# Splitting three of the last product's seven half-size products once more, in a float32 RWKV attention and Hadamard feed-forward kernel

## The chip, the cores and the metric

The kernel runs on one core of a Trainium2 chip, in float32 throughout. The metric is the device time of one execution in microseconds (us): the median over repeated runs. A profiled execution gives a trace of every instruction of the five engines: TensorE (PE, with its weight loads PEld), VectorE (DVE), ScalarE (ACT), GpSimd (POOL) and SyncE (SP), which issues all DMAs here.

## The reference, cut to what matters

```python
xn = _layernorm(x)                                   # x: 4 batches x 2048 tokens x 512 channels
r, k, v = (einsum(mix(xn, mu), W) for r, k, v)       # 512 x 512 each; mix = mu * x + (1 - mu) * the token before
attn = einsum(sigmoid(r) * wkv_recurrence(k, v, w, u), Wo)
up = silu(einsum(xn, W1)) * einsum(xn, W3)           # 512 -> 2048
ffn = einsum(fwht(up), W2)                           # Walsh-Hadamard over 2048, then 2048 -> 512
out = x + attn + ffn
```

The last step of each part is a product onto the same 512 channels. The kernel folds the Hadamard transform into `W2` once, puts `Wo` below it, and so computes one last product with 2048 + 512 = 2560 rows.

## The kernel before, in words

The 8192 tokens are worked in 8 blocks of `TB` = 1024 tokens. Within a block there are three stages on TensorE: the r, k and v projections, 16 turns of `up` (each makes 128 of the 2048 hidden channels for all 1024 tokens), and `down`, the last product. Meanwhile VectorE and ScalarE work through the recurrence (`wkv`, given out piece by piece by `step`).

Every product is done by the seven-product form of a 2 x 2 matrix product (Strassen-Winograd): weights and tokens are cut into halves, sums and differences of the quarters are made ("forms"), and seven products of half size take the place of eight. The forms of the weights are made by GpSimd in the first block and kept in DRAM (`part_w`, `down_w`). In `down` the contraction is cut into the halves kh (ten tiles of 128 rows each: eight of `hid`, two of `r_sb`), the output channels into the halves mh (two tiles of 128, index g), the tokens into two halves of 512. `y11`, `y12`, `y21`, `y22` are the quarters of the right-hand side (first index kh, second the token half). One of the seven products is 2 x 10 matmuls of 128 x 128 weights on 512 columns; a float32 matmul shows in the trace as two passes, each with its own weight load.

The order of work on each engine is the order of the program text (`InOrder`), and SP's queue is one such list for all DMAs. `product(k, ...)` inside `down` first issues the load of the weights of product k + 1 (1280 KB, into a ring `ring_b` of two slots), then lets the generator `between` do one part of the next block's preparation (`next_tokens`: statistics of the tokens, `normalize`, the mixed inputs `mixed` and their forms `mix_forms`), then issues its 20 matmuls. The differences of the y quarters stand between the products on VectorE, written in place. `normalize` gives two of the four channel tiles to VectorE and two to GpSimd. In the first block, `down_parts` and `down_forms` make the forms of the last product's weights during the first ten turns of `up`.

`pa`, `pb`, `pc` are PSUM banks that sums grow in; `act.copy` starts a second bank with what has been summed so far. `stage` and `x22_of` hold the residual x, which sums are added onto before they are stored. The last product of the last block is cut into two halves of 256 columns.

Of the kernel before, what the change touches and what calls it, by code (L numbers as in the profile page):

```python
# [14 lines left out]
P = 128  # L15
# [24 lines left out]
def tile_rwkv_attn_hadamard_ffn(  # L40
# [20 lines left out]
    NR = (NF + NB) // 2  # L61
    n_blocks = NT // TB
# [6 lines left out]
    ring_b = ctx.enter_context(tc.tile_pool(name="ring_b", bufs=2))  # L69
# [6 lines left out]
    down_w = dram.tile([7, P, NR, KH, P], F32, name="down_w")  # L76
# [3 lines left out]
    hid = const.tile([P, NF, TB], F32, name="hid")  # L80
    xnT = const.tile([P, NB, OFF + TB], F32, name="xnT")
    tf = const.tile([P, 4, KH, H], F32, name="tf")
    r_sb, k_sb, v_sb = (const.tile([P, NB, TB], F32, name=n) for n in ("r_sb", "k_sb", "v_sb"))
# [3 lines left out]
    turn = [0]  # L87

# [8 lines left out]
    u2_of = [e1b[:, ts(g, H)] for g in range(KH)]  # L97
    x22_of = [e1[:, ts(g, H)] for g in range(KH)]
    mix_of = {1: tf.rearrange("p f k t -> p (f k t)").rearrange("p (b t) -> p b t", t=TB)}
    mix_of[2], mix_of[0] = hid[:, 0:NB, :], hid[:, NB : 2 * NB, :]  # L100
    t4_of = {kind: hid[:, NF // 2 + n, :] for n, kind in enumerate((1, 2, 0))}
# [43 lines left out]
    def normalize():  # L145
        for b in range(NB):
            eng = dve if b < KH else pool
            for s, op in ((0, ALU.mult), (1, ALU.add)):
                xb = xnT[:, b, OFF : OFF + TB]
                eng.tensor_tensor(xb, xb, spread[:, s, :], op)  # L150
# [52 lines left out]
    def load_square(i, kind):  # L203
        t = ring_b.tile([P, NB, C], F32, tag="b", name=f"w_{i}_{kind}")
        sp.dma_start(out=t, in_=wrkv[kind])
        return t

    def projected(kind, w, h, half):
        pt = bank()
        for b in range(NB):  # L210
            pe.matmul(
                pt, lhsT=w[:, b, ts(h, P)], rhs=mix_of[kind][:, b, ts(half, H)], start=(b == 0), stop=(b == NB - 1)
            )
        dst = (r_sb, k_sb, v_sb)[kind][:, h, ts(half, H)]
        if kind == 0:
            act.activation(dst, pt, AF.Tanh, scale=0.5)
        else:
            act.copy(dst, pt)


    def wkv(h):
        w_h, u_h = weff[:, h : h + 1], vec[:, 4, h : h + 1]
        r, k, v = r_sb[:, h, :], k_sb[:, h, :], v_sb[:, h, :]
# [67 lines left out]
    def mix_forms(kind):  # L291

        m11, m12, m21, m22 = quarters(mix_of[kind], 0)
        if kind == 1:
            f1, f2 = (by_tile(s[:, OFF : OFF + TB]) for s in (sa, sb))
        else:
            slot = ring_b.tile([P, 2, KH, H], F32, tag="b", name=f"mf_{kind}")
            f1, f2 = slot[:, 0], slot[:, 1]
        f4 = by_tile(t4_of[kind])
        right_of[kind] = (m11, m21, m22, f1, f2, m12, f4)  # L300
        for out, x, y in ((f1, m12, m11), (f2, m22, f1), (m12, m22, m12), (f4, m21, f2)):
            dve.tensor_tensor(out, x, y, ALU.subtract)
            yield
# [61 lines left out]
    def projected_pair(i, n, w, tail, hook):  # L365
# [3 lines left out]
        dst = (r_sb, k_sb, v_sb)[kind]  # L369
        d11, d12, d21, d22 = (dst[:, mh * KH + g, ts(t, H)] for mh in range(2) for t in range(2))  # L370
# [25 lines left out]
    def up(i, j, w, tail, step):  # L396

        keep_parts(i, 3 * KH + j, w)
        h0, h1 = hid[:, j, 0:H], hid[:, j, H:TB]
# [24 lines left out]
    NP = NF // 2  # L424
    fold = [hid[:, NP + n, :] for n in range(NP)]

# [37 lines left out]
    def down_parts(n):  # L464
        t = ring_b.tile([P, 7, KH, P], F32, tag="b", name=f"df_{n}")
        if n >= NP:
            sp.dma_start(out=t[:, 0:4], in_=wo[n - NP])
        return t

    def down_forms(j, at, t):  # L470
        n, a = at[j] if j < NP else (j, None)
        far = down_w[:, :, n].rearrange("f p k c -> p f k c")
        if n < NP:
            a = a.rearrange("p (k m g c) -> p k m g c", k=2, m=2, c=P)
            seven_forms([t[:, f] for f in range(4)], a[:, 0, 0], a[:, 1, 0], a[:, 1, 1], a[:, 0, 1])
            sp.dma_start(out=far[:, 0], in_=a[:, 0, 0])
            sp.dma_start(out=far[:, 1:3], in_=a[:, 1])
            sp.dma_start(out=far[:, 3:7], in_=t[:, 0:4])
        else:
            forms_in(t)  # L480
            sp.dma_start(out=far, in_=t)

    def load_down(i, form):
        t = ring_b.tile([P, NR, KH, P], F32, tag="b", name=f"dw_{i}_{form}")
        sp.dma_start(out=t, in_=down_w[form])
        return t

    def rows(kh, half):

        n = NF // 2  # L490
        pieces = [hid[:, kh * n + 2 * a : kh * n + 2 * a + 2, ts(half, H)] for a in range(n // 2)]
        return pieces + [r_sb[:, kh * KH : (kh + 1) * KH, ts(half, H)]]

    order = (0, 1, 4, 6, 5, 3, 2)

    def down(i, w, between, w_after, last):
        y11, y12, y21, y22 = rows(0, 0), rows(0, 1), rows(1, 0), rows(1, 1)
        def product(k, pts, right, start, then):
            if k == 6:
                w_after()  # L500
            elif k:
                w.append(load_down(i, order[k + 1]))
            if k:
                next(between)
            for g in range(KH):
                whole = slice(0, H)
                for pt, cols in ending if last and k == 6 and g == KH - 1 else [(pts[g], whole)]:
                    for n in range(NR):
                        pe.matmul(
                            pt[:, cols], lhsT=w[k][:, n, g, :], rhs=right[n // 2][:, n % 2, cols],  # L510
                            start=start and n == 0, stop=n == NR - 1, skip_group_check=True,
                        )
                    then(g) if cols == whole else c21(g, pt, cols)

        def difference(out, x0, x1):
            for o, p0, p1 in zip(out, x0, x1):
                dve.tensor_tensor(o, p0, p1, ALU.subtract)
# [4 lines left out]
        def residual(slot, mh, g, half):  # L522
            c, t = at(mh, g, half)
            sp.dma_start(out=slot, in_=xT[c, t])

        def store(slot, mh, g, half):
            c, t = at(mh, g, half)
            sp.dma_start(out=outT[c, t], in_=slot)

        add = dve.tensor_tensor  # L530
        pa, pb, pc = ([bank() for _ in range(KH)] for _ in range(3))
        ending = [(pb[KH - 1], slice(0, H // 2)), (bank(), slice(H // 2, H))]
        s5 = [small.tile([P, H], F32, tag="s5", name=f"s5_{i}_d{g}") for g in range(KH)]
        for g in range(KH):
            residual(stage[g], 0, g, 0)
        product(0, pa, y11, True, lambda g: act.copy(pb[g], pa[g]))
        difference(y11, y12, y11)

        def c11(g):
            add(stage[g], pa[g], stage[g], ALU.add)  # L540
            store(stage[g], 0, g, 0)
            residual(stage[2 + g], 0, g, 1)
            residual(x22_of[g], 1, g, 1)

        product(1, pa, y21, False, c11)
        product(2, pc, y11, True, lambda g: act.copy(s5[g], pc[g]))
        difference(y12, y22, y12)
        for g in range(KH):
            add(x22_of[g], x22_of[g], s5[g], ALU.add)
        product(3, pc, y22, False, lambda g: None)  # L550
        difference(y22, y22, y11)

        def u2(g):
            act.copy(u2_of[g], pb[g])

        product(4, pb, y22, False, u2)
        difference(y21, y21, y22)
        for g in range(KH):
            add(u2_of[g], u2_of[g], stage[2 + g], ALU.add)
            add(stage[2 + g], pc[g], u2_of[g], ALU.add)  # L560
            store(stage[2 + g], 0, g, 1)
            residual(stage[g], 1, g, 0)

        def c22(g):
            add(x22_of[g], pb[g], x22_of[g], ALU.add)
            store(x22_of[g], 1, g, 1)
            if last and g == KH - 1:
                act.copy(ending[1][0][:, H // 2 :], pb[g][:, H // 2 :])

        product(5, pb, y12, False, c22)  # L570

        def c21(g, pt=None, cols=slice(0, H)):
            add(stage[g][:, cols], (pb[g] if pt is None else pt)[:, cols], stage[g][:, cols], ALU.add)
            c, t = at(1, g, 0)
            sp.dma_start(out=outT[c, t][:, cols], in_=stage[g][:, cols])

        product(6, pb, y21, False, c21)
# [29 lines left out]
    for i in range(n_blocks):  # L607
# [64 lines left out]
        w_down = []  # L672
        for j in range(NF):
# [6 lines left out]
            if j >= NF - 2:  # L680
                w_down.append(load_down(i, order[j - NF + 2]))
# [7 lines left out]
        def next_tokens():  # L689
# [7 lines left out]
            yield  # L697
# [3 lines left out]
            yield  # L701
# [3 lines left out]
            for _ in range(3):  # L705
                next(pending[2])
            yield

        def next_parts():
            if not last:  # L710
                parts.extend(load_parts(i + 1, n) for n in range(2))
# [3 lines left out]
        down(i, w_down, (None for _ in range(6)) if last else next_tokens(), next_parts, last)  # L715
# [53 lines left out]
```

## Time and profile before

| | |
|---|---|
| median of 3 runs (lowest to highest) | 3126.64 us (3126.60 to 3128.13) |
| profiled execution, its own time | 3126.89 us |
| its span, from first to last instruction | 3125.1 us |
| TensorE busy, share of span, passes | 3108.2 us, 99%, 7252 |
| VectorE busy | 2197.2 us, 70% |
| ScalarE / GpSimd busy | 873.9 us, 28% / 322.6 us, 10% |
| mean granted TensorE clock | 0.999 |
| DMA, mean over the span | 107 GB/s, 30.3% of 16 engines |

Lines of the views are read so: in groups of instructions, `x` is the count, then stand the busy time in us and the mean ns of one, then the idle time before them with what ended it. In the timeline, the start and the duration in us come first. All instructions carry line 34, that of the recording helper, so groups are told apart by tile names (output<-inputs). `SPq` is the issue of a DMA. PEclk is the granted clock of TensorE, as a share of the full one.

### The profile page before, as it was taken

Reading aid. Unit: us, or ns where it says so; the run is one execution under the profiler, and the core shown is the slowest. Engines: PE = TensorE matmul, PEld = TensorE weight load, DVE = VectorE, ACT = ScalarE, POOL = GpSimd, SP = SyncE. Lnnn points to the kernel's source line nnn. Section 1 sums busy time; section 2 is a strip of 40 time slices with the busy share of each in tenths; the row PEclk is TensorE's granted clock in tenths of the full one; section 3 lists DMA queues with packets and bytes.
Section 4 is the critical chain, followed back from the end, with each engine's and each line's share of the span. In section 5 each row is a group of like instructions: output and inputs, shape, how many; then the busy total and the mean of one; then the engine's idle time right before and its main releaser. Section 6 shows DMA issues by size and latency. Waiting matters only on the chain.

```text
span 3125.1 us, 20283 instructions
## 1 busy us (share of the span) xinstructions
PE 3108.2 (99%) x7252; PEld 1378.9 (44%) x7252; DVE 2197.2 (70%) x2317; ACT 873.9 (28%) x1375; POOL 322.6 (10%) x203
## 2 busy tenths in 40 slices
PE   8999999999999999999999999999999999999999
PEld 3444444444444444444444444444444444444444
DVE  6798847876478765797557965589564886658852
ACT  4233023330233203332123321333213331133310
POOL 3353131001100011000110001100011000010000
PEclk9999999999999999999999999999999999999999
DMA  4354433223322242222422233222332224322222
GB/s 163 104 183 162 161 116 110 77 109 135 108 77 76 103 153 96 76 78 107 150 93 78 75 133 123 97 75 79 136 135 78 79 74 160 111 84 73 80 97 78
DMA packets 75813, 334.45 MB, mean 107 GB/s; under 512 B 9152, under 2 KB 18624, under 8 KB 66368
## 3 DMA queue, kind: packets, MB, share of 16 engines
q1 hardware_dynamic: 75712, 333.15, 30.3%
q8 instruction: 58, 0.95, 0.1%
q14 instruction: 43, 0.35, 0.0%
HBM read 286.93 MB, written 46.19 MB: 107 GB/s over the span
## 4 chain that ended last, share of the span: by engine, by line
PE 99%; DVE 0%; DMA 0%; SPq 0%; issue 0%; ACT 0%; ACTq 0%
PE bank L34 99%; DVE xnT L34 0%; DMA hid<-w 0%; DVE tf L34 0%; SPq L34 0%; ACT tf L34 0%; ACT hid L34 0%; DVE v_sb L34 0%; ACTq L34 0%; ACT k_sb L34 0%
## 5 line engine op out<-in xcount | busy, mean ns | idle before, releaser
L34 PE MATMUL bank<-tf,part 128*128 128x512 f32 x2272 | 1042.2, 592 | 0.0
L34 PE MATMUL bank<-hid,dw 128*128 128x512 f32 (+1 forms) x1808 | 787.5, 588 | 0.0
L34 PE MATMUL bank<-xnT,part 128*128 128x512 f32 x1536 | 721.8, 592 | 0.0
L34 PEld LDWEIGHTS bank<-tf,part 128*128 128x128 f32 x2272 | 431.7, 190 | 543.4 <-issue 513.5
L34 ACT COPY bank<-bank 128x512 f32<-128x512 f32 x527 | 300.2, 570 | 1268.1 <-PE bank L34 1243.9
L34 PEld LDWEIGHTS bank<-hid,dw 128*128 128x128 f32 x1808 | 343.5, 190 | 426.0 <-issue 422.8
L34 PEld LDWEIGHTS bank<-xnT,part 128*128 128x128 f32 x1536 | 291.8, 190 | 367.4 <-issue 363.1
L34 DVE TENSOR_TENSOR hid<-hid 128x1024 f32<-128x1024 f32 (+1 forms) x173 | 221.8, 1310 | 105.2 <-PE bank L34 104.3
L34 DVE SCALAR_TENSOR_TENSOR hid<-hid,bank 128x512 f32<-128x512 f32 x256 | 174.0, 680 | 170.8 <-ACT hid L34 170.6
L34 PE MATMUL bank<-hid,part 128*128 128x512 f32 x616 | 271.2, 592 | 0.0
L34 DVE RECIPROCAL e1b<-e1b 128x512 f32<-128x512 f32 x64 | 214.1, 3347 | 1.1
L34 PE MATMUL bank<-r_sb,dw 128*128 128x512 f32 (+1 forms) x452 | 210.7, 588 | 0.0
L34 DVE TENSOR_TENSOR bank<-bank,s 128x512 f32<-128x512 f32 x256 | 168.0, 690 | 36.5 <-ACT bank L34 25.3
L34 ACT ACTIVATE hid<-bank 128x512 f32<-128x512 f32 x272 | 162.2, 600 | 94.0 <-PE bank L34 75.9
L34 PEld LDWEIGHTS bank<-hid,part 128*128 128x128 f32 x616 | 117.0, 190 | 147.3 <-issue 145.7
L34 DVE TENSOR_TENSOR hid<-hid,bank 128x512 f32<-128x512 f32 x256 | 173.6, 678 | 11.5 <-PE bank L34 7.1
L34 POOL TENSOR_TENSOR rs<-rs,neg_half 128x8 f32<-128x8 f32 x7 | 11.5, 1648 | 1581.1 <-DVE rs L34 1581.1
L34 DVE SCALAR_TENSOR_TENSOR hid<-xnT,vec,hid 128x1024 f32<-128x1024 f32 x64 | 93.1, 1489 | 97.2 <-ACT hid L34 97.2
L34 PEld LDWEIGHTS bank<-r_sb,dw 128*128 128x128 f32 x452 | 85.9, 190 | 106.4 <-issue 106.2
L34 ACT COPY s<-bank 128x512 f32<-128x512 f32 x128 | 75.0, 586 | 145.9 <-PE bank L34 145.9
L34 DVE TENSOR_TENSOR v_sb<-bank,v_sb 128x512 f32<-128x512 f32 (+1 forms) x33 | 22.1, 672 | 129.9 <-PE bank L34 129.9
L34 POOL TENSOR_TENSOR tf<-xnT 128x1024 f32<-128x1024 f32 x16 | 46.4, 2902 | 589.9 <-PE bank L34 589.9
(103 smaller groups left out, 2218.0 us busy)
## 6 DMA issues: line engine op xcount, KB each, us to landing
part<-part_w SPq DMA_DIRECT2D x148, 896.0 KB, 4.6
dw<-down_w SPq DMA_DIRECT2D x56, 1280.0 KB, 6.1
part_w<-part SPq DMA_DIRECT2D x22, 896.0 KB, 6.9
k_sb<-x SPq DMA_DIRECT2D x7, 2048.0 KB, 8.3
xnT<-xT SPq DMA_DIRECT2D x7, 2048.0 KB, 9.7
v_sb<-xT SPq DMA_DIRECT2D x48, 256.0 KB, 4.8
out<-v_sb SPq DMA_DIRECT2D x47, 256.0 KB, 2.1
part<-wpart SPq DMA_DIRECT2D x22, 512.0 KB, 5.0
```

What stands on the lines that cost most here:

```text
L34: return self.tc.keep_in_program_order(issue(*args, **kwargs))
```

## The change

Three of the seven products of `down` (those of forms 1, 4 and 6) are cut once more: contraction, output channels and columns are halved again, and seven products of five matmuls on 256 columns take the place of 20 matmuls on 512. They are called d0, d1 and d2 (class `Deep`, steps 0 to 6). Their steps are woven with each other and with the first plain product, in an order written out by hand; the other four products stay plain. All weights come in 37 pieces of 320 KB (128 x 5 x 128), through eight slots of `pieces_w`, each loaded seven pieces ahead (`load_piece`). A sum of a deep product begins on a PSUM bank that ScalarE has filled with zeros (`scale=0.0`). The right-hand forms of the deep products are made by VectorE each block; the second set of weight forms is made in the first block's turns 11 to 14 of `up` (`deep_forms`, by GpSimd, kept in `deep_w`). `hid` and `r_sb` become one tile `right`; `ring_b` is gone, its other users take halves of `pieces_w`. `normalize` runs wholly on VectorE, and the parts of `next_tokens` stand at four places in the new order. The diff, without the renaming:

```diff
     part_w = dram.tile([3 * KH + NF, P, 7, KH, P], F32, name="part_w")
-    down_w = dram.tile([7, P, NR, KH, P], F32, name="down_w")
+    down_w = dram.tile([2, 7, KH, P, QR, P], F32, name="down_w")
+    deep_w = dram.tile([3, 7, P, QR, P], F32, name="deep_w")
...
+    right = const.tile([P, 2, NR, TB], F32, name="right")
+    pieces_w = const.tile([P, 8, QR, P], F32, name="pieces_w")
...
     def normalize():
         for b in range(NB):
-            eng = dve if b < KH else pool
             for s, op in ((0, ALU.mult), (1, ALU.add)):
                 xb = xnT[:, b, OFF : OFF + TB]
-                eng.tensor_tensor(xb, xb, spread[:, s, :], op)
+                dve.tensor_tensor(xb, xb, spread[:, s, :], op)
...
+    PARTS = ((0, 0), (1, 0), (1, 1), (0, 1))
+    DEEP = (1, 4, 6)
+
+    def deep_forms(m):
+        t = pieces_w[:, 0:7]
+        for n, (rh, g) in enumerate(PARTS):
+            sp.dma_start(out=t[:, n], in_=down_w[rh, DEEP[m], g])
+        forms_in(t)
+        return t
 
-    order = (0, 1, 4, 6, 5, 3, 2)
+    def keep_deep(m, t):
+        sp.dma_start(out=deep_w[m].rearrange("f p q c -> p f q c"), in_=t)
...
+    def load_piece(u):
+        if u < len(program):
+            kind, form, n = program[u]
+            src = down_w[n[0], form, n[1]] if kind == "plain" else deep_w[form, DEEP_AT[n]]
+            sp.dma_start(out=pieces_w[:, (u + 7) % 8], in_=src)
...
+        def product(pt, rows, cols, start=False):
+            load_piece(u[0] + 7)
+            w = pieces_w[:, (u[0] + 7) % 8]
+            u[0] += 1
+            matmuls(pt, w, rows, cols, start)
...
+            def forms(self, *which):
+                q11, q12, q21, q22 = self.q
+                t1, t2, t3, t4 = self.t
+                for n in which:
+                    difference(*((t1, q12, q11), (t2, q22, t1), (t3, q22, q12), (t4, q21, t2))[n])
+
+            def step(self, n):
...
+                pt, rows, cols = (
+                    (a, q11, left), (f, t1, left), (b, t2, rest), (a, q22, rest), (a, q21, left), (b, t3, rest), (b, t4, left),
+                )[n]
+                if n < 2:
+                    act.activation(pt[:, cols], had_sb.unsqueeze(1).to_broadcast([P, 2, P]), AF.Copy, scale=0.0)
+                product(pt, rows, cols)
+                if n == 0:
+                    act.copy(b[:, rest], a[:, left])
+                elif n == 1:
+                    act.copy(self.s5, f[:, left])
+                elif n == 2:
+                    act.copy(a[:, rest], b[:, rest])
+                elif n == 5:
+                    act.copy(b[:, left], b[:, rest])
+
+            def onto(self, slots, g):
+                pt = (self.a, self.b)[g]
+                add(slots[g], pt)
+                dve.tensor_tensor(slots[g][:, rest], slots[g][:, rest], self.s5, ALU.add)
+
+        d0 = Deep(0, sets[0], y21, [*free, in_tf[0]])
+        d1 = Deep(1, sets[1], y11, [*in_k, in_tf[1]])
+        d2 = Deep(2, sets[0], y22, [*free, in_tf[2]])
...
+        d0.forms(0, 1, 2, 3)
+        plain_step(0, 0, (0, 0), True)
+        plain_step(0, 1, (0, 0), True)
+        next(between)
+        add(x11[0], pa[0])
+        d0.step(0)
+        d0.step(1)
+        plain_step(1, 0, (0, 0), True)
+        d0.step(2)
+        plain_step(1, 1, (0, 0), True)
+        add(x11[1], pa[1])
+        for q11, q12 in zip(y11, y12):
+            difference(q11, q12, q11)
+        d0.step(3)
+        d0.step(4)
+        d0.onto(x11, 0)
+        d0.step(5)
+        d1.forms(0)
+        d1.step(0)
+        d0.step(6)
+        d0.onto(x11, 1)
...
+        d1.forms(1)
+        d1.step(1)
+        d2.forms(0, 1)
+        d2.step(0)
+        d1.step(2)
+        d1.forms(2, 3)
+        d2.step(1)
+        d1.step(3)
+        d1.step(4)
+        d1.onto(x12, 0)
+        d1.onto(x22, 0)
+        d2.forms(2, 3)
+        d2.step(2)
+        d1.step(5)
+        next(between)
+        for q12, q22 in zip(y12, y22):
+            difference(q12, q22, q12)
+        d2.step(3)
+        d2.step(4)
+        d2.onto(x12, 0)
+        d2.step(5)
+        for rh in range(2):
+            for n in range(2):
+                difference(y22[2 * rh + n], y22[2 * rh + n], y11[2 * rh + n])
+        d1.step(6)
+        d1.onto(x12, 1)
+        d1.onto(x22, 1)
+        d2.step(6)
+        d2.onto(x12, 1)
...
+        plain_product((1, 1), c12)
+        for q21, q22 in zip(y21, y22):
+            difference(q21, q21, q22)
+        next(between)
+        plain_product((0, 1), c22)
+        next(between)
+        if not last:
+            plain_product((1, 0), c21)
...
             if j + 2 < NF:
                 parts.append(load_parts(i, 3 * KH + j + 2))
-            if j >= NF - 2:
-                w_down.append(load_down(i, order[j - NF + 2]))
+            if i == 0 and NR < j <= NR + 4:
+                if j > NR + 1:
+                    keep_deep(j - NR - 2, t)
+                if j < NR + 4:
+                    t = deep_forms(j - NR - 1)
+            if j == NF - 1:
+                for u in range(7):
+                    load_piece(u)
             tail = up(i, j, parts.pop(0), tail, step)
```

In the new order the first `next(between)` holds `token_before`, the load of the channels and the statistics; the second holds `normalize` alone; the third `mixed(1)` and three of its forms; the fourth `mixed(2)`, three of its forms and the loads of the next block's first two weight parts. `right` is indexed so that a quarter `quarter(kh, half, rh, cols)` is five row tiles (rh) of one kh, on 256 or 512 columns. In a y quarter's list `parts_of` the order is rh 0 left, rh 0 rest, rh 1 left, rh 1 rest; these four are q11, q12, q21 and q22 of a deep product.

## Prediction

> **What bounds the kernel now.** I read the page, then groups by shape, then the timeline where the change cuts in. The page and its chain of waits:
>
> ```profile
> PE 3108.2 (99%) x7252; PEld 1378.9 (44%) x7252; DVE 2197.2 (70%) x2317; ACT 873.9 (28%) x1375; POOL 322.6 (10%) x203
> ...
> PE 99%; DVE 0%; DMA 0%; SPq 0%; issue 0%; ACT 0%; ACTq 0%
> ```
>
> TensorE is the path from start to end: fewer columns is time saved, and every new wait of TensorE is time lost, since no slack takes it up. What a 256-column pass costs is seen in the last block's end (timeline):
>
> ```profile
> 3085.53 1.88 PE L34 MATMUL bank<-r_sb,dw 128*128 128x512 f32 x4
> ...
> 3087.25 7.03 PE L34 MATMUL bank<-hid,dw 128*128 128x512 f32 x16
> ...
> 3087.45 0.59 ACT L34 COPY e1b<-bank 128x512 f32<-128x512 f32 x1 [8.00 <-PE bank L34]
> ...
> 3113.00 3.62 PE L34 MATMUL bank<-hid,dw 128*128 128x256 f32 x16
> ...
> 3117.31 3.62 PE L34 MATMUL bank<-hid,dw 128*128 128x256 f32 x16
> ```
>
> 512 columns: (3087.25 - 3085.53) / 4 = 0.43 us a pass. 256 columns: (3117.31 - 3113.00) / 20 = 0.215, half, though each pass has its own weight load (190 ns). A result is out 0.16 us after the next pass starts (3085.53 + 1.88 = 3087.41), and ScalarE begins 0.04 us later. In a middle block's `down`, VectorE (timeline):
>
> ```profile
> 729.36 11.89 DVE L34 TENSOR_TENSOR xnT<-xnT,v_sb 128x1024 f32<-128x1024 f32 x4
> 741.17 4.62 DVE L34 TENSOR_TENSOR hid<-hid 128x1024 f32<-128x1024 f32 x4
> ```
>
> Beside GpSimd's half, `normalize` takes 2.97 us an operation; other operations of that size take 1.14 apiece in a row. Groups by shape and DMA issues give the other prices:
>
> ```profile
> L34 ACT COPY bank<-bank 128x256 f32<-128x256 f32 x1 | 0.4, 357 | 17.3 <-DVE e L34 17.3
> L34 DVE TENSOR_TENSOR v_sb<-bank,v_sb 128x256 f32<-128x256 f32 x2 | 0.8, 425 | 7.5 <-PE bank L34 7.5
> L34 POOL TENSOR_TENSOR part<-part 128x256 f32<-128x256 f32 x88 | 86.5, 994 | 164.1 <-DMA part<-wpart 121.7 <-PE bank L34 38.9
> L34 POOL TENSOR_TENSOR tf<-xnT 128x1024 f32<-128x1024 f32 x16 | 46.4, 2902 | 589.9 <-PE bank L34 589.9
> ```
>
> ```profile
> k_sb<-x SPq DMA_DIRECT2D x7, 2048.0 KB, 8.3
> xnT<-xT SPq DMA_DIRECT2D x7, 2048.0 KB, 9.7
> v_sb<-xT SPq DMA_DIRECT2D x48, 256.0 KB, 4.8
> ```
>
> **The matmuls: -50 us.** A block's `down` was 280 passes x 0.43 = 120.2 us (the timeline has 309.69 to 429.85). It becomes 160 x 0.43 + 210 x 0.215 = 113.9. Saved: 6.3 a block, 50 in 8. Weight loads stay under 0.215. A deep piece is 10 passes, 2.15 us.
>
> **The zero fills: +34 us.** In `step`, the fill of a bank stands on ScalarE's queue behind the copy of the step before, and that copy waits for TensorE to end that step. Where the next TensorE piece is the filled one, nothing covers it. The text has four such places: d0.step(1) behind d0.step(0); d1.step(0) behind the copy of d0.step(5); d2.step(0) behind d1.step(1); d2.step(1) behind d1.step(2). (d1.step(1) has d0.step(6) between; d0.step(0) has two plain pieces.) Each costs 0.16 result + 0.04 + copy 0.36 + fill + 0.04 + about 0.1 until passes run again. The fill is in no row: 0.30 (a copy pipelined behind another) to 0.5 (activations from SBUF take 0.72 on 512 columns); I take 0.37, near the 256 copy. Sum 1.07, ends 0.95 to 1.25; 32 x 1.07 = 34. ScalarE's other work is no cover: it is the queue itself.
>
> **VectorE alone normalizes, and where: +66 us.** Eight operations at 1.14 to 1.25 (the second of a pair needs the first): 9.6 us, less than VectorE's 11.9 now, so as an amount it is free. Its place decides. VectorE waits for d1.step(4) (`onto` reads its bank); from there its list until the first plain product after the weave can start is: d1 onto two slots, 2 x (0.60 + 0.46) = 2.1; two d2 forms of 1280 elements (1.14 x 1280 / 1024 = 1.41), 2.8; `normalize` 9.6; four y12 differences 5.6; d2 onto 1.1; the first two y22 differences 2.8, which `plain_step(0, 0, (1, 1))` reads. 24.0 us. TensorE from the same point has d2.2, d1.5, d2.3, d2.4, d2.5, d1.6, d2.6: seven pieces, 15.0. It waits 24.0 + 0.36 (result, start, restart) - 15.0 = 9.4 us. Last block: no `normalize`, 14.4 against 15.0, no wait. 7 x 9.4 = 66, ends 49 (7 each) and 77 (11 each, with 0.03 to 0.06 us between dependent operations). Behind the wait nothing is late: VectorE is then ahead of TensorE by a plain product. The other VectorE additions (ten forms, 2 adds for 1 per sum) stand in stretches where VectorE waits for TensorE and cost nothing; uncovered, the ten forms would be 14 a block. GpSimd loses work that nobody then waits for.
>
> **Queues.** SP issues 37 loads a block for 7, at 0.4 us: 15 of 114 us, hidden, since each is issued seven pieces ahead; a load lands in about 5 against the 15 to 30 that seven pieces last. The statistics' DMAs come a plain piece earlier than now, the next block's two part loads one product before their use (17 us against 4.6 to land): nothing. What SP's order can still do is rival C.
>
> **The second weight forms, block 0: +26 us.** Three rounds share one buffer (slots 0 to 6): read four pieces, make four forms, write 2240 KB, and only then the next. Reads: 256 KB rows land in 4.8, plus three issues of 0.4, so 6. Forms of 640 elements: between GpSimd's 0.99 (256) and 2.90 (1024), 1.95; four are 7.8. Write: the 2 MB rows, 8.3 to 9.7, so 9. A round is 23, three 69. They begin in turn 11 of `up`:
>
> ```profile
> 249.61 0.33 SPq L34 DMA_DIRECT2D part<-wpart  x1
> ...
> 309.69 2.74 PE L34 MATMUL bank<-hid,dw 128*128 128x512 f32 x6
> ```
>
> 250 + 69 = 319 at best; with GpSimd's part forms (3.0 to 5.8 a turn) and part loads between, 325. Piece 1 (slot 0) must then land, 329 or so; TensorE wants it at 309.7 + 4.3 = 314. It waits 15 (ends 8 and 26). Behind those loads on SP stand the next block's tokens (8.3), the statistics' way through DRAM, and behind these pieces 9 on: in other blocks the tokens are fetched some 12 us ahead of `down`, here after it, so I add 9 (0 to 12). `down_w` now lies in 512-byte runs: 2 more, as in turn 11 the part's forms end (250.6) hardly before they are used.
>
> **The clock: +17 us.** After the one gap of TensorE over 3 us now, the granted clock falls (timeline, then the windows view, where PEclk is the third number from the end: 0.51):
>
> ```profile
> 21.73 5.83 PE L34 MATMUL bank<-tf,w 128*128 128x512 f32 x9 [3.87 <-ACT hid L34]
> ...
> 22.90:26.40 3.50, 3.50 (x5) 1.35 (x4) 2.34 (x11) 1.45 (x4) 1.01 (x1) 0.51 1.03 410
> ```
>
> 3.4 us at half rate lose 1.7; the program's first passes, 0.85 apart from 8.86 to 12.41, lose 1.7 to 2.1. Nine waits of 9 us or more follow (seven and two in block 0): 9 x 1.9 = 17. Ends: 12 (the row's three slow passes alone, 1.3) and 31 (twice 1.7, if the clock needs as long again to rise). Waits of 1.07 us are like the 1.0 us gap at 44 us, after which the clock stayed.
>
> The Trainium skill ("TensorE: Matmul & The Clock Gate", Part 1) says that the clock halves after an idle window of about 3.4 us and comes back after a busy one, the windows running free. By that alone a restart could cost from one to two windows at half rate, an estimate of 1.7 to 3.4 us each, and the nine 15 to 31; the 1.9 of the rows lies at the low end. No rule there counts the 1 us waits.
>
> **Sum.** Profiled 3126.9 (span 3125.1, 1.8 around it; 0.25 above the median, which I neglect): 3126.9 - 50 + 34 + 66 + 26 + 17 = 3220.
>
> **The rivals.** (A) *Queues let later work pass* a waiting instruction, so fills run early and y22 differences go ahead of `normalize`. Place: ScalarE's fills and VectorE's list after d1.step(4). Left: -50 + 26 + 4 = 3107, faster. It decides if these waits sum below 2 us a block. Against: in every row above a wait ends in list order. 0.05. (B) *VectorE's list fits in the seven pieces* (a cheaper `normalize`, or VectorE not held by d1.step(4)): 66 and its 13 of clock go: 3141. For: the margin is a sum of small terms; against: it must shrink by 9.4 of 24. 0.11. (C) *Pieces come late in every block*: SP stands for the statistics before piece 9, and the readback's 1024 KB go ahead of it; 5 us x 7 and half their clock: 3220 + 35 + 6 = 3261. For: only a few us of slack; against: seven pieces lie ahead, 19 us from the start of piece 2. 0.14. (D) *Half-width passes don't keep 0.215 for long*: 0.25 would cost 7 a block, 3276. The end of the trace shows 40 in a row without. 0.02. The forecast keeps 0.68, with 3185 to 3250 as its own range.
>
> **How the numbers follow.** Own ends: VectorE 49 to 77, block 0 10 to 40, clock 12 to 31, fills 30 to 40. All low ends give 3178, all high 3265. The range 3165 to 3265 leaves out A, B and a little above: under 0.2. Only A and a part of B with a cheap block 0 could end below 3120: faster 0.05; within 0.2% (6 us, what a measurement here can tell) 0.03; slower 0.92.
>
> **What would show it.** Right: in each middle block one TensorE wait of 9 to 10 us released by VectorE's `right` between the weave and the first plain product; four of about 1 us released by ScalarE; deep passes 0.215 apart; `normalize` 1.2 us an operation; in block 0 some 25 us of waits for `pieces_w`; mean clock 0.993 to 0.996. Wrong: waits for DMA in middle blocks (C), or no VectorE wait (B).

## The result and the profile after

| | before | after |
|---|---|---|
| median, same chip (lowest to highest) | 3128.02 us (3126.60 to 3135.97) | 3232.40 us (3229.31 to 3233.23) |
| ratio after / before, 95% interval | | 1.0328 (1.0313 to 1.0343) |
| profiled execution: own time, span | 3126.89, 3125.1 us | 3233.2, 3231.4 us |
| mean granted TensorE clock | 0.999 | 0.984 |

The changed kernel is slower by 104 us; the prediction said 3220 us, with 3165 to 3265 as its range.

The page of the changed kernel, busy times and chain:

```profile
PE 3094.6 (96%) x7972; PEld 1520.8 (47%) x7972; DVE 2358.2 (73%) x2505; ACT 897.0 (28%) x1471; POOL 270.7 (8%) x187
...
PE 90%; DVE 6%; DMA 2%; POOL 1%; ACT 1%; issue 1%; SPq 0%; DVEq 0%; POOLq 0%; ACTq 0%
```

TensorE's share of the chain fell from 99% to 90%: the path now runs through other engines while TensorE stands still. Whom it waits for says the view of waits (engine, tile it writes, the releaser: us in total, times, longest):

```profile
PE bank L34 <- DVE right L34: 64.3, 7, 9.2
...
PE bank L34 <- ACT bank L34: 24.5, 32, 0.8
```

Seven waits for VectorE, one a block but the last, and 32 for ScalarE, four a block: both counts are those of the prediction. The timeline of VectorE in block 1 shows what the first kind waits for:

```profile
795.71 0.69 DVE L34 TENSOR_TENSOR v_sb<-bank,v_sb 128x512 f32<-128x512 f32 x1 [6.69 <-PE bank L34]
...
800.71 9.66 DVE L34 TENSOR_TENSOR xnT<-xnT,v_sb 128x1024 f32<-128x1024 f32 x8
810.29 5.69 DVE L34 TENSOR_TENSOR right<-right 128x1280 f32<-128x1280 f32 x4
...
817.02 5.69 DVE L34 TENSOR_TENSOR right<-right 128x1280 f32<-128x1280 f32 x4
```

VectorE begins with d1.step(4)'s sum at 795.71. From there it is never idle: the rest of d1's sums, two forms, `normalize` (9.66 us, 1.21 an operation), the y12 differences, d2 onto a slot, and at 817.02 the y22 differences. The second of these ends near 819.9. TensorE, same block (its line shows the shape of the first pass of a run):

```profile
788.93 8.90 PE L34 MATMUL bank<-right,pieces_w 128*128 128x256 f32 x40 [0.81 <-ACT bank L34]
...
806.30 4.48 PE L34 MATMUL bank<-tf,pieces_w 128*128 128x256 f32 x20
819.96 10.20 PE L34 MATMUL bank<-right,pieces_w 128*128 128x512 f32 x16 [9.18 <-DVE right L34]
```

The weave ends at 810.78 (806.30 + 4.48), and the plain product starts as the second y22 difference ends.

The second kind of wait, ahead of d2.step(0) in the same block, on ScalarE and on TensorE:

```profile
782.82 0.37 ACT L34 COPY s_d<-bank 128x256 f32<-128x256 f32 x1 [3.65 <-PE bank L34]
783.09 0.39 ACT L34 ACTIVATE bank<-had_sb 128x256 f32<-128x256 f32 x1
```

```profile
783.54 2.43 PE L34 MATMUL bank<-right,pieces_w 128*128 128x256 f32 x10 [0.75 <-ACT bank L34]
```

ScalarE's copy starts as TensorE ends the step before (782.79), the zero fill follows it, and TensorE's next pass starts 0.06 us after the fill's end.

What the wait for VectorE does to the clock is in the windows view (length, then busy time and count of PE, PEld, DVE, ACT and POOL, then PEclk):

```profile
815.93:826.17 10.24, 6.21 (x8) 2.57 (x9) 9.75 (x13) 0.00 (x0) 0.00 (x0) 0.50 0.01 2
```

The clock is at half for 10.24 us, the first four of them inside the wait, where it costs nothing. The passes after the wait start 0.85 us apart instead of 0.43.

Block 0, SP's and GpSimd's timeline around the second weight forms, and the first pass of `down`:

```profile
269.53 1.85 SPq L34 DMA_DIRECT2D pieces_w<-down_w  x4
...
295.79 1.75 SPq L34 DMA_DIRECT2D pieces_w<-down_w  x4
...
319.44 1.75 SPq L34 DMA_DIRECT2D pieces_w<-down_w  x4
...
336.42 0.37 SPq L34 DMA_DIRECT2D deep_w<-pieces_w  x1
```

```profile
347.96 12.41 PE L34 MATMUL bank<-right,pieces_w 128*128 128x512 f32 x28 [21.82 <-DMA pieces_w<-down_w]
```

Three rounds of read, form and write begin at 269.5, 295.8 and 319.4; the last write is issued at 336.4, and the first piece is there at 348: its load stands on SP behind that write. TensorE had been done with `up` at 326.

The account of the span, from the distances between the starts of successive passes (a pass's own 0.429 or 0.2145 us subtracted):

| term | predicted | measured |
|---|---|---|
| fewer columns | -50 | 3102.5 to 3051.0: -51.5 |
| zero fills | +34 | 24 of 0.92, 8 of 0.97, and each time 0.105 more at the second pass behind: +33.2 |
| VectorE's list, 7 waits | +66 | 7 x 9.36: +65.5 |
| block 0: first wait | +15 | +22.0 |
| block 0: tokens | +9 | 0 |
| block 0: turns of `up` | +2 | 2.1, 4.8, 1.2 and 2.8 in turns 9, 10, 11 and 15: +10.9 |
| passes at half rate after waits | +17 | +22.4 |
| the program's start | 0 | +2.3, less 1.2 as the first pass comes earlier |
| remainder, small delays of passes | 0 | +2.8 |

The measured terms sum to +106.4, and the spans differ by 106.3.

### The profile page after: what moved, and what is told of

The parts are those of the page before. It is cut to its first block, busy times and chain, and to the rows that moved or that the text cites. A ratio compares the mean times of both kernels' runs of the same rounds, so it can differ in the third digit from the quotient of the medians.

```text
span 3231.4 us, 22717 instructions
## 1 busy us (share of the span) xinstructions
PE 3094.6 (96%) x7972; PEld 1520.8 (47%) x7972; DVE 2358.2 (73%) x2505; ACT 897.0 (28%) x1471; POOL 270.7 (8%) x187
## 3 DMA queue, kind: packets, MB, share of 16 engines
q1 hardware_dynamic: 123696, 367.57, 33.5%
## 4 chain that ended last, share of the span: by engine, by line
PE 90%; DVE 6%; DMA 2%; POOL 1%; ACT 1%; issue 1%; SPq 0%; DVEq 0%; POOLq 0%; ACTq 0%
PE bank L34 90%; DVE right L34 2%; DVE xnT L34 2%; DMA part_w<-part 1%; POOL pieces_w L34 1%; ACT bank L34 1%; DMA pieces_w<-down_w 1%; DMA deep_w<-pieces_w 1%; DVE v_sb L34 0%; DMA part<-wpart 0%; DVE tf L34 0%; DVE e1b L34 0%; SPq L34 0%; POOL part L34 0%; DVE e L34 0%
## 5 line engine op out<-in xcount | busy, mean ns | idle before, releaser
L34 PE MATMUL bank<-right,pieces_w 128*128 128x512 f32 (+1 forms) x2628 | 895.1, 501 | 110.7 <-DVE right L34 64.3
L34 ACT COPY bank<-bank 128x512 f32<-128x512 f32 (+1 forms) x583 | 316.8, 543 | 1573.9 <-PE bank L34 1533.7
L34 PEld LDWEIGHTS bank<-right,pieces_w 128*128 128x128 f32 x2628 | 502.9, 193 | 500.4 <-issue 339.5
L34 DVE SCALAR_TENSOR_TENSOR right<-right,bank 128x512 f32<-128x512 f32 x256 | 174.0, 680 | 181.1 <-ACT right L34 180.9
L34 DVE TENSOR_TENSOR right<-right 128x1280 f32<-128x1280 f32 (+2 forms) x205 | 293.4, 1472 | 4.7 <-DMA part_w<-part 3.8
L34 PE MATMUL bank<-right,part 128*128 128x512 f32 x616 | 271.2, 592 | 0.0
L34 ACT ACTIVATE right<-bank 128x512 f32<-128x512 f32 x308 | 183.9, 600 | 120.4 <-PE bank L34 103.4
L34 PEld LDWEIGHTS bank<-right,part 128*128 128x128 f32 x616 | 117.0, 190 | 147.3 <-issue 145.2
L34 DVE TENSOR_TENSOR right<-right,bank 128x512 f32<-128x512 f32 x256 | 173.5, 678 | 11.5 <-PE bank L34 7.1
L34 POOL TENSOR_TENSOR part<-part 128x256 f32<-128x256 f32 x88 | 99.4, 1140 | 196.7 <-DMA part<-wpart 152.8
```

Of the source, the lines that this page charges most:

```text
L34: return self.tc.keep_in_program_order(issue(*args, **kwargs))
```

## The experiments

The theory: the result is four separate mechanisms (VectorE's list, in-order fills, the rounds in block 0, the clock), each of the size above. Each of the first runs takes one away.

**1. `normalize` behind the weave.** The one `next(between)` that holds it moves behind the last onto:

```diff
         d1.step(5)
-        next(between)
         for q12, q22 in zip(y12, y22):
...
         d2.onto(x12, 1)
+        next(between)
```

> The changed kernel with the place of normalize (the second of the four parts of next_tokens) moved from behind d1.step(5) to behind the last onto of the weave, just ahead of the first plain product after it; nothing is added or left out. Theory (place, not amount): VectorE's list after d1.step(4) is 14.4 us against 15.0 of TensorE, the seven waits of 9.36 us go (66 us), and with them their half-rate passes (about 2.3 us each, 16 us): 3232 - 82 = 3150, within 4 us. Rival (amount: VectorE has too much to do in down): the wait turns up later, at the differences or at the next block's first projections, and the time stays above 3210.

Measured: 3147.44 us, ratio 1.0063 (1.0046 to 1.0080), clock 0.994. Of the 85 us gained on the changed kernel 65.5 are the seven waits, 17.7 half-rate passes (22.4 to 4.7). Timelines of VectorE and TensorE in block 1 of this run:

```profile
801.80 9.66 DVE L34 TENSOR_TENSOR xnT<-xnT,v_sb 128x1024 f32<-128x1024 f32 x8
```

```profile
796.17 34.07 PE L34 MATMUL bank<-right,pieces_w 128*128 128x512 f32 x79
```

`normalize` takes the same 9.66 us, but TensorE runs 79 passes through it without a break. So the work was never too much; its place was wrong, as the prediction's sum had it.

**2. Both engines normalize, at the new place.**

```diff
     def normalize():
         for b in range(NB):
+            eng = dve if b < KH else pool
             for s, op in ((0, ALU.mult), (1, ALU.add)):
                 xb = xnT[:, b, OFF : OFF + TB]
-                dve.tensor_tensor(xb, xb, spread[:, s, :], op)
+                eng.tensor_tensor(xb, xb, spread[:, s, :], op)
```

> The changed kernel with normalize shared by VectorE and GpSimd again, as before the change, at its new place. Theory (place): four operations at 2.97 us beside GpSimd are 11.9 us against 9.66 alone, so the seven waits grow from 9.36 to about 11.6: 3232 + 16 = 3248. Rival (handing all of it to VectorE is what costs): half of the eight operations leave VectorE's list, the waits shrink to about 4.6 us each: 3232 - 33 = 3199, less some half-rate passes.

Measured: 3226.43 us, ratio 1.0316 (1.0300 to 1.0331): neither number. Timelines of GpSimd, VectorE and TensorE in block 1:

```profile
766.93 11.91 POOL L34 TENSOR_TENSOR xnT<-xnT,v_sb 128x1024 f32<-128x1024 f32 x4 [6.71 <-DMA v_sb<-stat_d]
```

```profile
770.44 11.14 DVE L34 TENSOR_TENSOR right<-right 128x1280 f32<-128x1280 f32 x4
...
804.54 4.87 DVE L34 TENSOR_TENSOR xnT<-xnT,v_sb 128x1024 f32<-128x1024 f32 x4
```

```profile
784.22 2.40 PE L34 MATMUL bank<-k_sb,pieces_w 128*128 128x256 f32 x10 [2.61 <-issue]
```

GpSimd's queue is empty, so its half starts as soon as the statistics land (766.9), 38 us before VectorE's half, and meets the y11 differences: four of these take 11.14 us instead of the 5.69 that four take alone. VectorE's half then runs undisturbed at 1.22 an operation. The wait at the weave's end shrinks from 9.36 to 4.57 (-33.5 in all), but a new wait of 2.8 to 2.9 a block, 5.1 and 3.8 in two, stands before the pass that reads the late form `k_sb` (+23.0; the view says "issue", the pass starts 0.1 us after VectorE's form ends), and half-rate passes rise from 22.4 to 28.5. The Trainium skill ("GPSIMD Engine Reference", 1. Specifications) says that GpSimd shares its SBUF interfaces with VectorE, with contention for VectorE operations that have two SBUF inputs; the differences are of that kind and agree, at 2.79 us on average against 1.42 alone.

**3. The fills ahead of the copies.** The four fills of d0 and d1 are issued before the weave, those of d2 before d1.step(1):

```diff
-                if n < 2:
-                    act.activation(pt[:, cols], had_sb.unsqueeze(1).to_broadcast([P, 2, P]), AF.Copy, scale=0.0)
...
         d0.forms(0, 1, 2, 3)
+        for d in (d0, d1):
+            for n in range(2):
+                d.fill(n)
...
         d1.forms(1)
+        for n in range(2):
+            d2.fill(n)
```

> The changed kernel with the six zero fills of a block issued ahead of the copies that held them: d0's and d1's before the first plain piece, d2's two before d1.step(1). Theory (queue order on ScalarE): the 32 waits of 0.92 to 0.97 us go, 30 us: 3202; the waits for VectorE's differences stay at 9.4. Rival (the restart of a deep product costs the time by itself, by the copy or by the bank): 3225 to 3232.

Measured: 3197.67 us, ratio 1.0221 (1.0206 to 1.0237): 34.7 less than the changed kernel (39.7 between the profiled executions), where the fills cost 33.2; four more are half-rate passes (18.2 for 22.4). The 32 waits for ScalarE are gone from the view of waits, the seven for VectorE stay, in one row with a short one of block 0:

```profile
PE bank L34 <- DVE right L34: 64.7, 8, 9.2
```

So a fill was never work that TensorE had to wait for; it stood behind a copy that waited for TensorE.

**4. Passes in the wait.** Ten matmuls of 512 columns, whose results nothing reads, fill most of each VectorE wait:

```diff
         d2.onto(x12, 1)
+        if not last:
+            for n in range(10):
+                pe.matmul(sets[1][2], lhsT=had_sb, rhs=right[:, 1, n, 0:H], start=True, stop=True, skip_group_check=True)
```

> The changed kernel with ten more matmuls (twenty passes of 0.43 us, 8.6 us) in each of the seven blocks that wait, right where TensorE waits for VectorE; they go into a bank that nobody reads again. Theory (the wait itself is VectorE's, and the clock falls because TensorE stands): the wait's end does not move, no half-rate passes follow it, 7 x 2.3 = 16 us less: 3216, granted clock near 0.99. Rival (the half-rate passes have another cause, such as the power of the 256-column passes): they stay, 3232. If the wait is not an idle one at all: 3232 + 60.

Measured: 3215.07 us, ratio 1.0281 (1.0266 to 1.0296), 17.3 below the changed kernel, clock 0.995. Timeline of TensorE in block 1:

```profile
807.64 8.75 PE L34 MATMUL bank<-right,had_sb 128*128 128x512 f32 x20
817.00 23.44 PE L34 MATMUL bank<-right,pieces_w 128*128 128x512 f32 x54 [0.61 <-DVE right L34]
```

The wait still ends with VectorE's second y22 difference, 0.61 us after the added passes, and the passes that follow run at full rate. Half-rate passes fall to 6.0 us, all of them in block 0. The clock's part of the loss is thus caused by TensorE standing still, and is separate from the wait.

**5. Shorter rounds in block 0.** The raw parts of a deep weight are read from `down_w` when needed, so a round writes four made forms and not seven, and its fourth part lies in slot 7:

```diff
-        t = pieces_w[:, 0:7]
-        for n, (rh, g) in enumerate(PARTS):
-            sp.dma_start(out=t[:, n], in_=down_w[rh, DEEP[m], g])
-        forms_in(t)
-        return t
+        at = [pieces_w[:, s] for s in (0, 1, 2, 7)]
+        for a, (rh, g) in zip(at, PARTS):
+            sp.dma_start(out=a, in_=down_w[rh, DEEP[m], g])
+        seven_forms([pieces_w[:, s] for s in range(3, 7)], *at)
+        return pieces_w[:, 3:7]
...
-        sp.dma_start(out=deep_w[m].rearrange("f p q c -> p f q c"), in_=t)
+        sp.dma_start(out=deep_w[m, 3:7].rearrange("f p q c -> p f q c"), in_=t)
...
             kind, form, n = program[u]
+            if kind == "deep" and DEEP_AT[n] < 3:
+                form, n = DEEP[form], PARTS[DEEP_AT[n]]
+                kind = "plain"
```

> The changed kernel with shorter rounds for the second weight forms in block 0: the three raw parts of a deep product are read by the pieces straight from down_w, so a round writes only the four made forms (1280 KB for 2240), and the fourth part is read into slot 7, so that a round's reads need not wait for the write before. Theory (three serial rounds are late): a round goes from 24 to 26 us to about 16 (forms 8 to 9, then the write or the reads beside them, 6 to 7), three end some 25 us earlier, and of the 22.0 us wait ahead of down in block 0 about 5 or less is left: 3232 - 18 = 3214, with its half-rate passes perhaps 3212. Rival (TensorE waits there for VectorE's recurrence or for SP's other loads): the wait stays above 15 us, 3225 or more.

Measured: 3220.03 us, ratio 1.0294 (1.0278 to 1.0310): 12.4 below the changed kernel. The first wait of `down` is 12.8 us, not 5 or less. SP's timeline has the reads at 285.07 and 306.29, behind the first and second writes, so the first two rounds last 17.6 and 21.2 us and not 16: the next reads are issued with the write, but in the second round the forms, which need all four, begin only at 294.71, 9.6 us after the first was issued (7.1 in the same round of the changed kernel), and GpSimd's four forms take 11.1 us there, where VectorE works beside it. The direction was right, and the price of a round, once more, too low.

**6. Longer runs.** `down_w` laid out so that the first forms are written in runs of 1 KB instead of 512 bytes (its reads and writes are indexed to match):

```diff
-    down_w = dram.tile([2, 7, KH, P, QR, P], F32, name="down_w")
+    down_w = dram.tile([2, 7, P, QR, KH, P], F32, name="down_w")
```

> The changed kernel with down_w laid out so that its writes in block 0 are again of 1024-byte runs; in exchange the pieces that lie in down_w are read in 512-byte runs. Theory (the short runs hold up the queue that the first block's weight parts stand in): the waits of 2.1, 4.8 and 1.2 us in turns 9 to 11 of up go, with half-rate passes after them about 10 us: 3222. Rival (these turns were at their limit before, and GpSimd's forms beside VectorE, 5.6 us for 4.0, tip them over): the waits stay, 3230 to 3236. A bad end: reads in 512-byte runs come late in every block, 3240 or more.

Measured: 3231.45 us, ratio 1.0329 (1.0313 to 1.0345), no different from the changed kernel. The waits in turns 9 to 11 stay (1.6, 4.1 and 1.6). The runs' length is not what delays them, though the prediction had put 2 us down to it.

**7. SP's part load ahead of its writes, in block 0.** This asks where the turns' waits come from, and why the rounds start at 269.5 and not at the 250 of the prediction:

```diff
-                down_forms(j, folded, t)
+                kept = down_forms(j, folded, t)
+                next(kept)
             if j + 2 < NF:
                 parts.append(load_parts(i, 3 * KH + j + 2))
+            if i == 0 and j < NR:
+                next(kept, None)
```

(In `down_forms` a `yield` stands between the forms and their writes.)

> In block 0 SyncE writes a turn's made forms of the down weight to memory only after it has issued the load of the next raw part, so that the load no longer stands behind GpSimd's forms on SyncE. Theory (the turns of up in block 0 run at 14.8 us against 12.0 of TensorE because the part load queues behind GpSimd's forms): the waits of 2.1, 4.8 and 1.2 us in turns 9 to 11 go, the rounds of late pieces start some 10 us earlier than 267 to 269 us, and the wait ahead of down shrinks by 8 to 10 from 22; 3232 - 20 = 3212. Rival (GpSimd's own forms beside VectorE are the limit, not the load's place on the queue): the waits in turns 9 to 11 stay within 1 us each and the time is 3228 or more.

Measured: 3213.69 us, ratio 1.0277 (1.0260 to 1.0294): 18.7 below the changed kernel. SP's timeline of this run, the loads of the parts, and TensorE's first pass of `down`:

```profile
225.27 0.33 SPq L34 DMA_DIRECT2D part<-wpart  x1
...
237.29 0.33 SPq L34 DMA_DIRECT2D part<-wpart  x1
...
249.31 0.33 SPq L34 DMA_DIRECT2D part<-wpart  x1
249.69 1.85 SPq L34 DMA_DIRECT2D pieces_w<-down_w  x4
```

```profile
326.86 13.44 PE L34 MATMUL bank<-right,pieces_w 128*128 128x512 f32 x30 [16.33 <-DMA pieces_w<-down_w]
```

The loads of turns 9, 10 and 11 go out every 12.0 us, the length of a turn, and the waits of those turns are gone. In the changed kernel the same three were issued at 253.98, 262.84 and 269.14, since up to turn 9 the load stands on SP behind the write of `down_w`, which waits for GpSimd's forms. The rounds begin at 249.7, and the first wait is 16.5 us. It shrank by 5.5 and not by 8 to 10, because `down` is reached 16 us earlier too.

**8. Three mends together:** the edits of runs 1, 3 and 5.

> The changed kernel with three edits together: normalize behind the weave, the zero fills issued early, the shorter rounds in block 0. If the costs are separate and add up: 3232 - 85 (normalize, measured alone) - 35 (fills, measured alone) - 18 (rounds, expected alone) = 3094, which is 33 us, 1%, below the kernel before. If the gains overlap (a wait that was hidden under another comes up): 3110 to 3130.

Measured: 3106.27 us, ratio 0.9929 (0.9914 to 0.9944): faster than the kernel before. By the single runs it would be 3232.4 - 85.0 - 34.7 - 12.4 = 3100. Six of that are missing, as much as one new wait of 3.2 us ahead of d0.step(1) and 3.1 of half-rate passes behind it. The view says "issue", but the pass starts at 347.26, 0.1 us after VectorE's form for it ends:

```profile
345.67 1.48 DVE L34 TENSOR_TENSOR right<-right 128x1280 f32<-128x1280 f32 x1
```

So VectorE is already the next to be waited for. Besides, block 0 has still 2.1, 4.8, 1.3 and 2.2 in `up` and 8.2 ahead of `down`.

**9. Four mends:** run 8 and the edit of run 7.

> The three mends together (normalize late, fills ahead of copies, short rounds), and SyncE's part loads ahead of its writes. If the load's place on the queue was the limit of block 0's turns: 3106 less 8 for the waits in turns 9 to 11 and less 6 to 8 of the wait ahead of down, about 3091. Rival: VectorE, which is some 10 us behind TensorE when down of block 0 begins, becomes the next to be waited for there, and the time is 3098 or more. If GpSimd's forms are the limit: 3106.

Measured: 3095.30 us (3094.95 to 3095.43), ratio 0.9896 (0.9881 to 0.9911): 32.8 us below the kernel before, clock 0.998. It lies between the two numbers, because both theories are partly right. The waits in the turns and for pieces fall to 3.0 in all, and VectorE's wait ahead of d0.step(1) grows from 3.2 to 12.5, since TensorE reaches it 21 us earlier and VectorE's form comes only 11 us earlier. Timelines of TensorE and VectorE in block 0:

```profile
335.87 9.44 PE L34 MATMUL bank<-right,pieces_w 128*128 128x256 f32 x26 [12.38 <-issue]
```

```profile
322.94 6.57 DVE L34 RECIPROCAL e1b<-e1b 128x512 f32<-128x512 f32 x2
...
334.28 1.48 DVE L34 TENSOR_TENSOR right<-right 128x1280 f32<-128x1280 f32 x1
```

d0.step(1) reads the form that VectorE makes at 334.28, behind the last part of the recurrence. Of the 51.5 us of fewer columns, 12.5 + 3.0 + 1.8 (half-rate passes) are given back there; nearly all the rest is kept. Whether that last wait can go was not tried.

## Why the prediction was right, and where it was not

**The columns.** Right: -50 against -51.5. 256-column passes start 0.2145 us apart also inside `down`. Over that the 1680 more of them lose 5.6 us, but 3.4 of it are the 32 passes, one behind each fill, that start 0.105 us late; the others lose 1.3 ns a pass.

**VectorE's list.** Right to half a microsecond: 66 against 65.5. Both sides of the sum hold: VectorE was predicted 24.0 from d1.step(4)'s sum to the second y22 difference, TensorE 15.0; the trace has 24.2 (795.71 to 819.9) and 15.1 (795.7 to 810.8). The seven waits themselves rule out rival B, and run 1 shows that the place and not the amount sets them. The prediction's own price, `normalize` at 1.2 apiece with GpSimd idle, is in the row of 9.66.

**The fills.** The mechanism was right and so was the price: 0.92 to 0.97 each and the 0.105 behind it, 1.02 to 1.08, against 1.07 (the prediction had 0.1 in it until passes run again). The fill took 0.39 for the assumed 0.37, but its start overlaps the end of the copy by 0.1. Run 3 shows the cause.

**Rivals A, C and D.** A would need VectorE's or ScalarE's list to let later work pass; the 39 waits end in list order. C needed waits for DMA in middle blocks; there is none. D needed deep passes well over 0.2145; 5.6 us over 1680 passes are 3.3 ns, far from the 35 it reckoned with.

**Block 0.** This step was mis-sized: 26 predicted, 33 measured, and its parts are wrong by more than the sum. It started the rounds at 250 and they started at 269.5, for two reasons. The row shown for it, the part load at 249.61, is that of turn 10 (turns counted from 0, the last such load is turn 13's); turn 11's is at 256.01. And the turns of `up` did not keep their old times. GpSimd's timeline has the first forms of the last product in the kernel before, and then in the changed one:

```profile
106.32 1.18 POOL L34 TENSOR_TENSOR df<-e 128x256 f32<-128x256 f32 x1 [26.62 <-issue]
```

```profile
116.20 0.72 POOL L34 TENSOR_TENSOR pieces_w<-e 128x256 f32<-128x256 f32 x1 [35.38 <-PE bank L34]
```

The forms now lie in `pieces_w`, and the first waits for TensorE, which still reads that buffer. SP's write of them goes from 110.92 to 119.23, and the lag is kept and grows: turn 9's write goes from 240.96 to 253.51, and turn 11's load from 256.01 to 269.14. Turns 9 to 11 wait 8.1 us for it (the view puts 2.1 of that to VectorE here, and to the part load in runs 2, 4 and 5). The prediction let this buffer's new users pass without a cost. Run 7 shows that the loads' place behind the writes hands the lag on to TensorE; that the buffer starts it is read from the trace alone, and was not tried apart, and why the lag grows is open.

That the first wait of `down` missed by only 7 is in part luck, since errors cancel. The rounds started 19.5 us late and took 78.4 us until TensorE could begin, where the prediction reckoned 79 until piece 1; TensorE itself came to `down` 16.4 later than the prediction had it. Nor did TensorE work through the first piece (slot 7) meanwhile, for which the prediction took off 4.3: SP issued that load only behind the third write, and the first pass of `down`, at 347.96, waits for it. So 19.5 - 0.6 - 16.4 + 4.3 = 6.8.

The 9 for tokens that come late never showed: VectorE waits 1.9 us for `k_sb`, and nothing of TensorE's stands close behind the statistics. The 2 us for short runs is refuted by run 6.

**The clock.** The direction was right, the price of one restart low: 16.9 / 7 = 2.4 us for a VectorE wait and 5.5 in block 0 beside it, against nine of 1.9. The mean clock, 0.984, was missed clearly (0.993 to 0.996): it counts the half-rate stretch inside the wait, which no pass feels. Seven stretches of 10.24, 20.48 in block 0, 6.83 at the start and two of 3.41 are 106 us at half; 1 - 0.5 x 106 / 3231 = 0.984. So a mean clock alone is no measure of time lost.

The Trainium skill's rule ("TensorE: Matmul & The Clock Gate", Part 1) of free-running windows of 3.4 us agrees: 10.24 and 20.48 are three and six of 3.41. The prediction's estimate from it, 1.7 to 3.4 a restart, holds the 2.4 of the VectorE waits. That a whole window has to be idle does not hold here: in turn 15 of the changed kernel a wait of 2.8 us is followed by 3.4 us at half rate (314.17 to 317.59) that cost 1.8, while five waits of 2.8 to 2.9 in run 2 are followed by none.

**The sum.** 3220 against 3232.4: of the profiled miss of 13 us, block 0 is 7, half-rate passes 5, the remainder 3, the start 1; columns, fills and VectorE take back 3.

## What to carry to other kernels

When TensorE is the whole path, price a split by the other engines' lists: from the sum that an engine must take off a bank to the operation that frees TensorE's next input, count both lists and compare. An operation that itself waits, or whose result is needed only later, must not stand ahead of one that TensorE needs next, on any queue: here a copy ahead of a fill, `normalize` ahead of differences, a write ahead of a load. Three of the four mends were changes of order alone, and together the four turned 3.3% slower into 1.0% faster.

## What the runs showed that was not expected

- A wait of half the length costs as much clock. In run 2 a wait of 4.57 us is followed by six passes 0.85 apart, 2.6 us lost; after 9.36 us four to seven passes are slow, 1.8 to 3.1 lost. In the wait of run 2 the half rate lasts 6.8 us, two thirds of the 10.24. The waits of about 1 us are followed by no half rate.
- An idle engine runs ahead: GpSimd's half of `normalize` started 38 us before VectorE's, and hurt an operation that is elsewhere in the text (5.69 to 11.14 us for four).
- Reads that SP issued directly behind a write of 1280 KB, without waiting for it, took longer: in run 5's second round the forms could begin 9.6 us after the first of the four was issued, against 7.1 in the changed kernel, where the reads wait until the write has landed.
